# Moving one table in SBUF and regrouping rows in DRAM: a convolution followed by a Laplace-type spectral layer

## The chip, the cores and the metric

The kernel runs on one core of a Trainium2 chip. A core has five engines that run side by side, each through its own list of instructions: TensorE (PE, matrix products, with the loading of weights shown apart as PEld), VectorE (DVE), ScalarE (ACT), GpSimd (POOL) and SyncE (SP, which here only issues DMA transfers). Sixteen DMA engines move data between DRAM and SBUF, the on-chip memory of 128 partitions. [...] The metric is device time in microseconds (us) of the whole kernel; lower is better.

## The reference

All data are float32. `x` has 16 images of 16 channels of 256 by 256 points. Two residual layers follow each other, each on group-normalised input:

```python
x = x + _L0_conv_ref(_gn(x), L0_conv_weight)
x = x + _L1_conv_ref(_gn(x), ty, tx, weights_pole1, weights_pole2, weights_residue)

def _L1_conv_ref(x, ...):
    alpha = fft2(x)
    A = 1.0 / (omega1 - weights_pole1);  Bm = 1.0 / (omega2 - weights_pole2)
    S = einsum('ikpq,oikp,xikq->oxik', weights_residue, A, Bm)
    output_residue1 = einsum('biox,oxik->bkox', alpha, S)
    C = einsum('biox,oikp->bikpx', alpha, A)
    D = einsum('bikpx,xikq->bikpq', C, Bm)
    output_residue2 = einsum('bikpq,ikpq->bkpq', D, weights_residue)
    x1 = ifft2(output_residue1).real
    F = einsum('kbpq,bipz->kbiqz', output_residue2, E1)   # E1, E2: exp(pole * t)
    x2 = einsum('kbiqz,biqx->kizx', F, E2).real
    return x1 + x2 / Nx / Ny
```

`_gn` is a group norm over pairs of channels without scale. `_L0_conv_ref` comes to a 3 by 3 circular convolution over 16 channels. `_L1_conv_ref` takes a two-dimensional Fourier transform, mixes the 16 channels at each frequency with a weight built from poles and residues, adds a low-rank transient part, and transforms back.

## The kernel before

The kernel runs in four stages, one after the other, with scratch tensors in DRAM between them.

**Convolution** (`conv`, one call per step g, 24 steps per image, 384 in all). `load_x` brings an image in as two halves of 18 rows per partition, each in four loads (`PARTS`, `load_part`, L123); the loads for image b + 2 are issued while image b is convolved. Per step 16 pairs of matmuls (L294) run with 32 by 32 weights. Every six steps two PSUM tiles of rows `lo` and two of the mirrored rows `hi` are finished; ScalarE evicts them (L309) into `vt`. `mirror` then makes the sum and the difference of a row and its mirror image: the sum on VectorE into `vsum` (L261), the difference on GpSimd in place (L264); ScalarE squares both for the second norm (L272). The list `folded` says at which later step SP stores which half of them (L319) into `vD[b]`, one scratch tensor per image with the sums and the differences 2 MB apart. `x_stats` computes the first norm's statistics (L179) in pieces spread over the steps before an image. A generator, `tables`, is advanced by one `next` per step and builds the pole tables meanwhile: `make_hat` runs over two sides and two halves, loads `s_h` from `hD` for each (L439, eight loads that each fill 16 partitions with five rows of 2 KB), and a few steps later ScalarE squares it (L452). `make_c` writes the residues' table to `cD`.

**Fold** (64 units of a channel i and four images). `load_v` reads sums and differences of a unit into `s` (L729, one load per image, two units ahead; those of the first unit are issued by GpSimd), `fold` folds them along x on VectorE and GpSimd (L740 to L754), `lines` and `columns` transform them on PE (L762, L770, L790, L805) through the tile `t`, and VectorE and GpSimd write the spectrum `spec` of a channel, which is stored to `aD` (L961). Even and odd channels have a `spec` buffer of their own, and there are two buffers of `t`. The first weights of the next stage (`weights`, tiles `u` and `v`) are computed in its last units.

**Mix** (32 groups g). `ct` is loaded from `cD` in one transfer of 4 MB (L995). `sums` multiplies weights by `ct` on PE (L1017), `spread` copies the result into `sg` on ScalarE and VectorE (L1034, L1037), `mix` multiplies `sg` by `abd`, blocks of `aD` (L1087, L1092, L1105), and the results are evicted to `yt` and stored to `yD` (L1119). `first_sums` is the start of this stage: all four pieces of the first `sg` before the first `mix`.

**Last stage** (64 units of a channel k and four images). `load_v` reads the same sums and differences into `vl` (L1295), `combine` joins the halves of `yD` on GpSimd (L1312, L1316), `along_x` and `along_y` transform back (L1348, L1372, L1373), `put_out` adds `vl` (L1381), makes top and bottom rows from sum and difference (L1383, L1384) and stores them (L1386).

Pools of tiles are placed in SBUF one behind the other, and those of a new stage take bytes of the old one; the first write or load of a new tile waits for whoever last used any of its bytes. In this build `t` lies at 119,904 to 144,480 of each partition, even `spec` at 144,480 to 177,248, and `ct` at 142,368 to 175,136. An engine works through its list in order: a wait at its head holds up everything behind it, SP's DMA issues included.

Of the kernel before, what the change touches and what calls it, by code (L numbers as in the profile page):

```python
# [16 lines left out]
B = 16  # L17
# [7 lines left out]
def conv_then_laplace_kernel(ctx: ExitStack, tc: tile.TileContext, a: dict, out: bass.AP):  # L25
# [39 lines left out]

    vD = [dp.tile([2, P, C, N], FP, name=f"vD{b}", tag=f"vD{b}") for b in range(B)]
    aD = dp.tile([P, 2 * C, N * B], FP, name="aD", tag="aD")
# [41 lines left out]
    xp = p1.enter_context(tc.tile_pool(name="xt", bufs=5))  # L109
    vp = p1.enter_context(tc.tile_pool(name="vt", bufs=6))  # L110
    fp = p1.enter_context(tc.tile_pool(name="v_sums", bufs=2))
    jp = p1.enter_context(tc.tile_pool(name="junk", bufs=1))
# [6 lines left out]

    PARTS = 0, 5, 9, 14, 18  # L120

    def load_part(t, b, h, i, j):
        nc.sync.dma_start(out=t[:, i:j], in_=x[b][:, 16 * h + i : 16 * h + j])  # L123

# [133 lines left out]

    def mirror(g, b, u, lo, hi):
        both = fp.tile([P, 2, 2, N], FP, name="vsum", tag="vsum")  # L260
        nc.vector.scalar_tensor_tensor(  # L261
            both, lo, 1.0, hi, ALU.mult, ALU.add, accum_out=sums[:, b, u : u + 1]
        )
        nc.gpsimd.tensor_tensor(lo, lo, hi, ALU.subtract)  # L264
        folded.extend((g + 4 + 2 * j + r, b, u, j, t, r) for j, t in enumerate((both, lo)) for r in range(2))
        squared.append((g + 5, lambda: square(both, 4 + 2 * u, b, bias=shift2[:, b : b + 1])))
        squared.append((g + 7, lambda: square(lo, 5 + 2 * u, b)))

    def square(t, col, b, **by):

        junk = jp.tile([P, 4 * N], FP, name="junk", tag="junk")
        nc.scalar.activation(  # L272
            junk,
            t.rearrange("p r j x -> p (r j x)"),
            AF.Square,
            accum_out=sums[:, b, col : col + 1],
            **by,
        )

    def conv(g):  # L280


        for c in range(4):
            for r in range(4):
                at = g if r < 2 else g - 3
                if not 0 <= at < 24 * B:
                    continue
                b, u, n = at // 24, at // 6 % 4, at % 6
                phase, tap = n // 3, n % 3
                if n == 0 and c == 0:  # L290
# [3 lines left out]
                nc.tensor.matmul(  # L294
                    acc[r][32 * c : 32 * c + 32],
                    lhsT=ready[b][0][rows, phase, tap],
                    rhs=halves[b][u // 2][rows, q : q + 5 : 4, 2 - tap : 2 - tap + N],
                    start=n == 0,
                    stop=n == 5,
                )  # L300
        for r in (0, 1) if g % 6 == 5 else (2, 3) if g % 6 == 2 else ():
            at = g if r < 2 else g - 3
            if not 0 <= at < 24 * B:
                continue
            b, u = at // 24, at // 6 % 4
            if r % 2 == 0:
                vt = vp.tile([P, 2, 2, N], FP, name="vt", tag="vt")
                acc["v", r // 2] = vt
            nc.scalar.activation(vt[:, r % 2], acc[r], AF.Identity, bias=ready[b][1])  # L309
            if r == 3:  # L310
                later.append((g + 2, lambda g=g, b=b, u=u, lo=acc["v", 0], hi=vt: mirror(g, b, u, lo, hi)))
        while later and (later[0][0] <= g or g >= 24 * B + 2):
            later.pop(0)[1]()
        while squared and (squared[0][0] <= g or g >= 24 * B + 2):
            squared.pop(0)[1]()
        while folded and (folded[0][0] <= g or g >= 24 * B + 2):
            _, b, u, j, t, r = folded.pop(0)
            y = 64 * r + 16 * u
            nc.sync.dma_start(  # L319
                out=vD[b][j, y : y + 16].rearrange("(t y) c x -> (y c) t x", t=2),  # L320
                in_=t[:, r],
            )
# [96 lines left out]
    def make_hat(side):  # L419
# [13 lines left out]
        for half in range(2):  # L433
# [3 lines left out]
            at = slice(half * n, half * n + n)  # L437
            for p0 in range(0, P, 16):
                nc.sync.dma_start(  # L439
                    out=five[p0 : p0 + 16, 0:5],  # L440
                    in_=hD[0:5, side, :, at].rearrange("j a n -> a j n"),
                )
# [271 lines left out]
    prp = pool(p1, "prod", 2)  # L714
    bp = pool(p1, "b_const")
    pa = pool(p1, "p_y", 3, space=PSUM)
    px = pool(p1, "p_x", 4, space=PSUM)
# [139 lines left out]
    kp = pool(p2, "m_const", side="right")  # L857
    up = pool(p2, "uv", side="right")

# [20 lines left out]
    def weights(g):  # L880

        shape = [P, 32, 4]
        u = up.tile([P, 4, 32, 4], FP, name="u", tag="u")
        w, den, e, f = (u[:, j] for j in range(4))
        pr2, pre, pim = (prU[:, j].unsqueeze(2).to_broadcast(shape) for j in range(3))
        nc.vector.tensor_tensor(
            w,
            omg[:, g].unsqueeze(1).to_broadcast(shape),  # L890
            pims.unsqueeze(2).to_broadcast(shape),
            ALU.subtract,
        )
# [8 lines left out]
        v = up.tile([P, 32, 2, 4], FP, name="v", tag="v")  # L902
# [70 lines left out]
    wp = pool(p2, "w", 2)  # L973
    ep = pool(p2, "exps")
    a1 = pool(p2, "abd2")
    zp = pool(p2, "between")
# [62 lines left out]
    def first_sums():  # L1039
# [8 lines left out]
        sg = new_sg(0)  # L1048
        other = up.tile([P, 2, 2 * C], FP, name="other", tag="other")
        for h, w in enumerate((wt, w128)):  # L1050
# [328 lines left out]
    def put_out(k, b0, r, vl):  # L1379

        nc.vector.scalar_tensor_tensor(r, vl, 0.5, r, ALU.mult, ALU.add)  # L1381
        ol = op.tile([P, 2, 4, N], FP, name="ol", tag="ol")
        nc.vector.tensor_tensor(ol[:, 0], r[:, 0], r[:, 1], ALU.add)  # L1383
        nc.vector.tensor_tensor(ol[:, 1], r[:, 0], r[:, 1], ALU.subtract)  # L1384
# [28 lines left out]
    for n, (k, b0) in enumerate(units):  # L1413
# [7 lines left out]
        if n + 1 < len(units):  # L1421
# [4 lines left out]
            load_ahead(n + 1)  # L1426
        r = rp.tile([P, 2, 4, N], FP, name="r", tag="r")
        for j in range(4):
# [3 lines left out]
            if j == 0 and n:  # L1432
                put_out(*done)
            last = (ey_now[:, j], hs[:, j], pt, r[:, :, j], begun[j])
        done = (k, b0, r, v_now)
# [97 lines left out]
def _laid_out(x, L0_conv_weight, L1_conv_ty, L1_conv_tx, L1_conv_weights_pole1, L1_conv_weights_pole2, L1_conv_weights_residue):  # L1533
# [7 lines left out]
    rows = np.concatenate([np.pad(rows, ((0, 0), (0, 0), (1, 0))), np.pad(N - 1 - rows, ((0, 0), (0, 0), (0, 1)))])  # L1541
    g["x"] = xp[:, :, rows % N].transpose(0, 2, 3, 1, 4, 5).reshape(-1, P, 34, N + 2)
    w = np.asarray(L0_conv_weight)
# [52 lines left out]
```

## Time and profile before

| | us |
|---|---|
| median of 3 runs | 2668.16 |
| lowest and highest run | 2650.97, 2669.53 |
| the profiled execution's own time | 2673.96 |
| its span in the trace | 2672.0 |
| PE busy | 2486.5 (93%) |
| VectorE busy | 1994.7 (75%) |
| ScalarE busy | 1448.0 (54%) |
| GpSimd busy | 1311.7 (49%) |
| moved by DMA | 653.18 MB, 476,828 packets |

Times within the trace are counted from the start of the span. A group of instructions is named by its line, its engine and its operation, then output tile and input tiles. A number in brackets behind an instruction is the time that its engine had been idle, and what ended it; "issue" stands for an idle time whose end the profile can't put down to another engine. The chain of waits follows the work that ended last back through what released it. PE's clock is granted in windows; a figure below 1.00 means that some ran at half speed. The trace also has one record per DMA packet, with its size and duration.

### The profile page before, as it was taken

How to read it: one execution, taken by the hardware profiler on the slowest of the kernel's cores; microseconds unless marked ns; L12 is line 12 of the kernel's file. 1: busy time of each engine (PE TensorE's matmuls, PEld its weight loads, DVE VectorE, ACT ScalarE, POOL GpSimd, SP SyncE). 2: the span in 40 equal slices, each digit the busy share in tenths (PEclk: the TensorE clock that was granted, in tenths of full speed). 3: DMA queues.
4: the chain of work that ended last, by engine and by line, in shares of the span. 5: the costliest groups of instructions: out<-in, count | busy, mean ns of one | idle time of the engine just before them, and what ended most of it. 6: DMA issues, size and time to landing. Idle time of an engine off the chain costs nothing.

```text
span 2672.0 us, 84459 instructions
## 1 busy us (share of the span) xinstructions
PE 2486.5 (93%) x35314; PEld 1882.8 (70%) x35314; DVE 1994.7 (75%) x3805; ACT 1448.0 (54%) x2727; POOL 1311.7 (49%) x1181
## 2 busy tenths in 40 slices
PE   5988899889999999996999999999699999999998
PEld 2444454457777777774778878788588888888887
DVE  7767688848888888886777878888367666766666
ACT  2565566565666666664666656666244444444443
POOL 1333368433333333333466655676546565565653
PEclk9999999999999999998999999999899999999999
DMA  7888978855557656654777777777889989898985
GB/s 272 277 278 274 278 253 278 290 197 181 206 198 250 225 203 206 247 195 174 216 225 223 230 222 221 229 226 232 229 281 294 286 286 289 280 294 282 292 281 178
DMA packets 476828, 653.18 MB, mean 244 GB/s; under 512 B 51062, under 2 KB 426998, under 8 KB 466592
## 3 DMA queue, kind: packets, MB, share of 16 engines
q1 hardware_dynamic: 475376, 640.58, 74.6%
q8 instruction: 278, 4.55, 0.7%
q0 software_dynamic: 928, 3.02, 0.4%
q10 hardware_dynamic: 144, 4.19, 0.4%
q14 instruction: 102, 0.84, 0.1%
HBM read 368.15 MB, written 280.36 MB: 243 GB/s over the span
## 4 chain that ended last, share of the span: by engine, by line
PE 68%; DMA 12%; DVE 10%; SPq 5%; issue 3%; ACT 2%; POOL 0%; DVEq 0%; ACTq 0%; POOLq 0%
PE ps_conv L294 16%; PE ps_mix L1105 11%; PE ps_y L762 9%; PE ps_y L770 8%; PE ps_p L1348 5%; PE ps_x L805 4%; PE ps_f L1372 4%; PE ps_f L1373 4%; DMA yk<-yD 4%; DMA yD<-yt 3%; PE ps_s L1017 3%; DVE r L1381 2%; SPq L1119 2%; DMA out_y<-ol 2%; PE psd L790 1%
## 5 line engine op out<-in xcount | busy, mean ns | idle before, releaser
L1105 PE MATMUL ps_mix<-abd,sg 128*64 128x128 f32 x8192 | 484.5, 277 | 36.2 <-ACT yt L1218 14.5
L1105 PEld LDWEIGHTS ps_mix<-abd,sg 128*64 128x64 f32 x8192 | 454.4, 139 | 89.3 <-ACT yt L1218 47.8
L1312 POOL TENSOR_TENSOR u<-yk 128x512 f32<-128x512 f32 (+1 forms) x268 | 348.9, 1333 | 307.5 <-PE ps_p L1348 200.8
L294 PE MATMUL ps_conv<-xt,wc 32*32 32x512 f32 x12288 | 451.4, 618 | 48.5 <-issue 44.0
L294 PEld LDWEIGHTS ps_conv<-xt,wc 32*32 32x32 f32 x12288 | 252.6, 104 | 235.3 <-issue 157.9
L778 ACT ACTIVATE t<-ps_y,vmr 128x384 f32<-128x384 f32 x512 | 297.0, 580 | 163.9 <-PE ps_y L770 163.9
L1037 DVE STREAM_SHUFFLE sg<-ps_s 128x512 f32<-128x512 f32 (+1 forms) x264 | 328.8, 1317 | 0.0
L762 PE MATMUL ps_y<-tabE,vq 128*128 128x256 f32 x1024 | 313.5, 388 | 13.2 <-DVE vq L751 11.7
L264 POOL TENSOR_TENSOR vt<-vt 128x1024 f32<-128x1024 f32 x64 | 151.6, 2369 | 330.6 <-DVE vsum L261 268.5
L770 PE MATMUL ps_y<-tabO,vq 128*128 128x256 f32 x1024 | 306.4, 381 | 0.0
L1348 PEld LDWEIGHTS ps_p<-inv,u 128*128 128x128 f32 x2048 | 266.0, 193 | 50.2 <-issue 25.1
L1372 PE MATMUL ps_f<-pt,inv 128*128 128x256 f32 x1008 | 300.9, 380 | 0.0
L1373 PE MATMUL ps_f<-hs,ey 128*128 128x256 f32 x1008 | 300.0, 379 | 0.0
L1376 DVE TENSOR_TENSOR r<-ps_f,q 128x256 f32<-128x256 f32 x256 | 107.0, 418 | 252.4 <-ACT q L1375 252.4
L1348 PE MATMUL ps_p<-inv,u 128*128 128x128 f32 x2048 | 279.4, 280 | 13.2 <-POOL u L1316 13.1
L1034 ACT ACTIVATE sg<-ps_s,mcol 128x512 f32<-128x512 f32 (+1 forms) x264 | 179.5, 689 | 201.9 <-DVE sg L1037 117.9
L309 ACT ACTIVATE vt<-ps_conv,xq 128x512 f32<-128x512 f32 x256 | 161.9, 683 | 196.3 <-PE ps_conv L294 196.2
L762 PEld LDWEIGHTS ps_y<-tabE,vq 128*128 128x128 f32 x1024 | 189.8, 191 | 89.9 <-ACT q L818 51.2
L1375 ACT COPY q<-ps_f 128x256 f32<-128x256 f32 x256 | 95.4, 372 | 289.3 <-PE ps_f L1373 285.5
L750 POOL TENSOR_TENSOR vq<-vf 128x512 f32<-128x512 f32 x64 | 81.4, 1272 | 294.2 <-DVE vf L754 277.3
L1350 ACT COPY pt<-ps_p 128x512 f32<-128x512 f32 x256 | 150.1, 586 | 136.1 <-PE ps_p L1348 131.5
L770 PEld LDWEIGHTS ps_y<-tabO,vq 128*128 128x128 f32 x1024 | 195.7, 191 | 27.0
(238 smaller groups left out, 4072.1 us busy)
## 6 DMA issues: line engine op xcount, KB each, us to landing
yD<-yt SPq DMA_DIRECT2D x512, 128.0 KB, 3.5
vl<-vD SPq DMA_DIRECT2D x256, 256.0 KB, 4.0
out_y<-ol SPq DMA_DIRECT2D x128, 512.0 KB, 9.8
s<-vD SPq DMA_DIRECT2D x252, 256.0 KB, 5.9
aD<-spec SPq DMA_DIRECT2D x15, 4096.0 KB, 13.2
yk<-yD SPq DMA_DIRECT2D x60, 1024.0 KB, 8.7
xt<-in_x SPq DMA_DIRECT2D x64, 645.0 KB, 5.3
xt<-in_x SPq DMA_DIRECT2D x64, 516.0 KB, 7.0
```

Source lines behind the costliest of these rows:

```text
L294: nc.tensor.matmul(acc[r][32 * c : 32 * c + 32], lhsT=ready[b][0][rows, phase, tap], rhs=halves[b][u // 2][rows, q : q + 5 : 4, 2 - tap : ...
L309: nc.scalar.activation(vt[:, r % 2], acc[r], AF.Identity, bias=ready[b][1])
L762: nc.tensor.matmul(ps[:, 0:N], lhsT=vf[:, xo, 0, j], rhs=tabE[:, 0 : i + 2 : i + 1], start=True, stop=False, skip_group_check=True,)
L770: nc.tensor.matmul(ps[:, P : P + N], lhsT=vf[:, xo, 1, j], rhs=tabO[:, i : C + 1 : C - i], start=False, stop=True, skip_group_check=True,)
L778: nc.scalar.activation(t[:, xo, j].rearrange("p l n -> p (l n)"), ps[:, 0:384], AF.Copy, scale=vmr[:, 0, b0 + j, i : i + 1],)
L1034: nc.scalar.activation(to[..., k : k + 2], src[odd], AF.Copy, scale=nsgn)
L1037: nc.vector.stream_shuffle(to[..., C + k : C + k + 2], src[1 - odd], swap)
L1105: nc.tensor.matmul(ps[64 * t : 64 * t + 64, j], lhsT=sg[:, f : f + 2].rearrange("p f m -> p (f m)"), rhs=abd[jq][:, :, 2 * t + cc, 2 * jj ...
L1312: nc.gpsimd.tensor_tensor(u[:, :, j].rearrange("p b (c n) -> p c b n", c=8), in0, in1, o)
L1348: nc.tensor.matmul(ps[:, at], lhsT=u[:, n], rhs=tab, start=True, stop=True)
L1372: nc.tensor.matmul(ps[:, e], lhsT=tab, rhs=pt[:, e], start=True, stop=False)
L1373: nc.tensor.matmul(ps[:, e], lhsT=ey[:, e], rhs=hs, start=False, stop=True)
```

## The change

Four things change together.

- The single buffers `u` and `v` of `weights` leave the right end of SBUF: the first `u` sits in a pool `u0` of the fold, the later ones in a pool `u` below `abd2`. The tiles above it move up: `ct` now lies at 144,672 to 177,440.
- Sum and difference of a unit of the convolution share a tile `pair`, and `vD` is one tensor per four images in which a row of a channel holds, for four images, sum and difference side by side. A store writes runs of 2 KB, and `s` and `vl` are read in runs of 4 KB per partition, by two loads a unit. The output has the same order, by pairs of images.
- `x` is laid out in groups of two rows (2,064 bytes) with 16 bytes between them, and `PARTS` is made even.
- A batch of `s_h` is five loads over 128 partitions with a broadcast source, one per row, instead of eight over 16 partitions.

```diff
-    vD = [dp.tile([2, P, C, N], FP, name=f"vD{b}", tag=f"vD{b}") for b in range(B)]
+    vD = [dp.tile([P, C, 4, 2, N], FP, name=f"vD{b}", tag=f"vD{b}") for b in range(B // 4)]
...
-    vp = p1.enter_context(tc.tile_pool(name="vt", bufs=6))
-    fp = p1.enter_context(tc.tile_pool(name="v_sums", bufs=2))
+    vp = p1.enter_context(tc.tile_pool(name="v_pair", bufs=3))
+    fp = p1.enter_context(tc.tile_pool(name="v_far", bufs=2))
...
-    PARTS = 0, 5, 9, 14, 18
+    PARTS = 0, 4, 10, 14, 18

     def load_part(t, b, h, i, j):
-        nc.sync.dma_start(out=t[:, i:j], in_=x[b][:, 16 * h + i : 16 * h + j])
+        nc.sync.dma_start(
+            out=t[:, i:j].rearrange("p (n r) x -> p n (r x)", r=2),
+            in_=x[b][:, 8 * h + i // 2 : 8 * h + j // 2, 0 : 2 * (N + 2)],
+        )
...
-    def mirror(g, b, u, lo, hi):
-        both = fp.tile([P, 2, 2, N], FP, name="vsum", tag="vsum")
+    def mirror(g, b, u, pair, hi):
+        both, lo = pair[:, :, :, 0], pair[:, :, :, 1]
...
         nc.gpsimd.tensor_tensor(lo, lo, hi, ALU.subtract)
-        folded.extend((g + 4 + 2 * j + r, b, u, j, t, r) for j, t in enumerate((both, lo)) for r in range(2))
+        folded.extend((g + 7 + r, b, u, pair, r) for r in range(2))
...
-            nc.scalar.activation(vt[:, r % 2], acc[r], AF.Identity, bias=ready[b][1])
+            if r == 0:
+                pair = vp.tile([P, 2, 2, 2, N], FP, name="pair", tag="pair")
+                acc["v", 0] = pair, pair[:, :, :, 1]
+            elif r == 2:
+                far = fp.tile([P, 2, 2, N], FP, name="far", tag="far")
+                acc["v", 1] = far, far
+            to = acc["v", r // 2][1]
+            nc.scalar.activation(to[:, r % 2], acc[r], AF.Identity, bias=ready[b][1])
...
             nc.sync.dma_start(
-                out=vD[b][j, y : y + 16].rearrange("(t y) c x -> (y c) t x", t=2),
-                in_=t[:, r],
+                out=vD[b // 4][y : y + 16, :, b % 4].rearrange("(t y) c h x -> (y c) t (h x)", t=2),
+                in_=pair[:, r].rearrange("p t h x -> p t (h x)"),
             )
...
-            for p0 in range(0, P, 16):
+            for j in range(5):
                 nc.sync.dma_start(
-                    out=five[p0 : p0 + 16, 0:5],
-                    in_=hD[0:5, side, :, at].rearrange("j a n -> a j n"),
+                    out=five[:, j],
+                    in_=hD[j, side, :, at].unsqueeze(0).to_broadcast([8, 16, n]),
                 )
...
-        s = sp.tile([P, 2, 4, N], FP, name="s", tag="s")
-        for j in range(4):
-            eng.dma_start(
-                out=s[:, :, j], in_=vD[b0 + j][:, :, i, :].rearrange("h y x -> y h x")
-            )
-        return s
+        s = sp.tile([P, 4, 2, N], FP, name="s", tag="s")
+        for j in range(0, 4, 2):
+            eng.dma_start(out=s[:, j : j + 2], in_=vD[b0 // 4][:, i, j : j + 2])
+        return s.rearrange("p b h x -> p h b x")
...
-    up = pool(p2, "uv", side="right")
+    up = {"v": pool(p2, "v", side="right"), "u0": u0}
...
-        u = up.tile([P, 4, 32, 4], FP, name="u", tag="u")
+        u = up["u" if g else "u0"].tile([P, 4, 32, 4], FP, name="u", tag="u")
...
     ep = pool(p2, "exps")
+    up["u"] = pool(p2, "u")
     a1 = pool(p2, "abd2")
...
-        vl = vp.tile([P, 2, 4, N], FP, name="vl", tag="vl")
-        for j in range(4):
-            nc.sync.dma_start(
-                out=vl[:, :, j], in_=vD[b0 + j][:, :, k, :].rearrange("h y x -> y h x")
-            )
+        vl = vp.tile([P, 4, 2, N], FP, name="vl", tag="vl")
+        for j in range(0, 4, 2):
+            nc.sync.dma_start(out=vl[:, j : j + 2], in_=vD[b0 // 4][:, k, j : j + 2])
...
-        for h in range(2):
-            nc.sync.dma_start(
-                out=out[k, b0 : b0 + 4, h].rearrange("b y x -> y b x"), in_=ol[:, h]
-            )
+        for j in range(0, 4, 2):
+            nc.sync.dma_start(out=out[k, b0 // 4, :, j : j + 2], in_=ol[:, j : j + 2])
```

The host's preparation of `x` and its reading of the output follow the new order; both only move data.

More of the change, by code (lines that the diff above doesn't have):

```diff
@@ L269, in square @@
     def square(t, col, b, **by):
-        junk = jp.tile([P, 4 * N], FP, name="junk", tag="junk")
+        junk = jp.tile([P, 4, N], FP, name="junk", tag="junk")
         nc.scalar.activation(
             junk,
-            t.rearrange("p r j x -> p (r j x)"),
+            t.rearrange("p r j x -> p (r j) x"),
             AF.Square,
@@ L305, in conv @@
             b, u = at // 24, at // 6 % 4
-            if r % 2 == 0:
-                vt = vp.tile([P, 2, 2, N], FP, name="vt", tag="vt")
-                acc["v", r // 2] = vt
-            nc.scalar.activation(vt[:, r % 2], acc[r], AF.Identity, bias=ready[b][1])
+            if r == 0:
[6 more added lines that the diff above has]
+            nc.scalar.activation(to[:, r % 2], acc[r], AF.Identity, bias=ready[b][1])
             if r == 3:
-                later.append((g + 2, lambda g=g, b=b, u=u, lo=acc["v", 0], hi=vt: mirror(g, b, u, lo, hi)))
+                later.append((g + 2, lambda g=g, b=b, u=u, pair=acc["v", 0][0], hi=to: mirror(g, b, u, pair, hi)))
         while later and (later[0][0] <= g or g >= 24 * B + 2):
@@ L316, in conv @@
         while folded and (folded[0][0] <= g or g >= 24 * B + 2):
-            _, b, u, j, t, r = folded.pop(0)
+            _, b, u, pair, r = folded.pop(0)
             y = 64 * r + 16 * u
             nc.sync.dma_start(
-                out=vD[b][j, y : y + 16].rearrange("(t y) c x -> (y c) t x", t=2),
-                in_=t[:, r],
+                out=vD[b // 4][y : y + 16, :, b % 4].rearrange("(t y) c h x -> (y c) t (h x)", t=2),
+                in_=pair[:, r].rearrange("p t h x -> p t (h x)"),
             )
@@ L715, in conv_then_laplace_kernel @@
     bp = pool(p1, "b_const")
+    u0 = pool(p1, "u0")
     pa = pool(p1, "p_y", 3, space=PSUM)
@@ L901, in weights @@
         yield
-        v = up.tile([P, 32, 2, 4], FP, name="v", tag="v")
+        v = up["v"].tile([P, 32, 2, 4], FP, name="v", tag="v")
         nc.vector.tensor_tensor(v[:, :, 0], e, den, ALU.mult)
@@ L1048, in first_sums @@
         sg = new_sg(0)
-        other = up.tile([P, 2, 2 * C], FP, name="other", tag="other")
+        other = up["u"].tile([P, 2, 2 * C], FP, name="other", tag="other")
         for h, w in enumerate((wt, w128)):
@@ L1381, in put_out @@
         nc.vector.scalar_tensor_tensor(r, vl, 0.5, r, ALU.mult, ALU.add)
-        ol = op.tile([P, 2, 4, N], FP, name="ol", tag="ol")
-        nc.vector.tensor_tensor(ol[:, 0], r[:, 0], r[:, 1], ALU.add)
-        nc.vector.tensor_tensor(ol[:, 1], r[:, 0], r[:, 1], ALU.subtract)
-        for h in range(2):
-            nc.sync.dma_start(
-                out=out[k, b0 : b0 + 4, h].rearrange("b y x -> y b x"), in_=ol[:, h]
-            )
+        ol = op.tile([P, 4, 2, N], FP, name="ol", tag="ol")
+        nc.vector.tensor_tensor(ol[:, :, 0], r[:, :, 0], r[:, :, 1], ALU.add)
+        nc.vector.tensor_tensor(ol[:, :, 1], r[:, :, 0], r[:, :, 1], ALU.subtract)
+        for j in range(0, 4, 2):
+            nc.sync.dma_start(out=out[k, b0 // 4, :, j : j + 2], in_=ol[:, j : j + 2])
     units = [(k, b0) for k in range(C) for b0 in range(0, B, 4)]
@@ L1426, in conv_then_laplace_kernel @@
             load_ahead(n + 1)
-        r = rp.tile([P, 2, 4, N], FP, name="r", tag="r")
+        r = rp.tile([P, 4, 2, N], FP, name="r", tag="r")
         for j in range(4):
@@ L1433, in conv_then_laplace_kernel @@
                 put_out(*done)
-            last = (ey_now[:, j], hs[:, j], pt, r[:, :, j], begun[j])
+            last = (ey_now[:, j], hs[:, j], pt, r[:, j], begun[j])
         done = (k, b0, r, v_now)
@@ L1541, in _laid_out @@
     rows = np.concatenate([np.pad(rows, ((0, 0), (0, 0), (1, 0))), np.pad(N - 1 - rows, ((0, 0), (0, 0), (0, 1)))])
-    g["x"] = xp[:, :, rows % N].transpose(0, 2, 3, 1, 4, 5).reshape(-1, P, 34, N + 2)
+    xr = xp[:, :, rows % N].transpose(0, 2, 3, 1, 4, 5).reshape(-1, P, 17, 2 * (N + 2))
+    g["x"] = np.pad(xr, ((0, 0), (0, 0), (0, 0), (0, 4)))
     w = np.asarray(L0_conv_weight)
@@ L1589 @@
         args[name] = nc.dram_tensor(f"in_{name}", v.shape, mybir.dt.from_np(v.dtype), kind="ExternalInput").ap()
-    out = nc.dram_tensor("out_y", (C, B, 2, P, N), FP, kind="ExternalOutput").ap()
+    out = nc.dram_tensor("out_y", (C, B // 4, P, 4, 2, N), FP, kind="ExternalOutput").ap()
     with tile.TileContext(nc) as tc:
@@ L1593 @@
     r = run_bass_kernel_spmd(nc, [arrays], core_ids=[0])
-    y = r.results[0]["out_y"].transpose(1, 0, 2, 3, 4)
+    y = r.results[0]["out_y"].transpose(1, 3, 0, 4, 2, 5).reshape(B, C, 2, P, N)
     return np.concatenate([y[:, :, 0], y[:, :, 1, ::-1]], 2)
```

## The prediction

> **What bounds the kernel now.** I first cut the span into its stages (busy microseconds by engine in each stretch, then the granted clock, the DMA share and GB/s).
>
> ```profile
> 47.00:592.00 545.00, 488.26 (x12304) 267.57 (x12299) 393.21 (x790) 327.92 (x593) 248.77 (x188) 0.97 0.82 266
> 592.00:602.00 10.00, 2.19 (x5) 1.31 (x5) 4.26 (x10) 1.48 (x3) 2.48 (x2) 0.50 1.07 355
> 602.00:1218.00 616.00, 615.50 (x4096) 443.15 (x4096) 524.28 (x1205) 372.55 (x644) 221.02 (x281) 1.00 0.58 207
> 1218.00:1254.00 36.00, 14.09 (x288) 8.50 (x296) 19.66 (x88) 10.14 (x33) 11.34 (x8) 0.72 0.68 264
> 1254.00:1895.00 641.00, 604.79 (x12176) 514.72 (x12160) 504.04 (x905) 407.06 (x680) 389.62 (x298) 0.98 0.76 223
> 1895.00:1938.00 43.00, 24.32 (x197) 20.30 (x184) 15.99 (x16) 10.62 (x26) 29.67 (x43) 0.84 0.82 228
> 1938.00:2662.00 724.00, 718.53 (x5936) 617.41 (x5928) 494.32 (x686) 312.95 (x742) 408.60 (x360) 1.00 0.88 279
> ```
>
> The first busy figure is PE. Fold (602 to 1218) and the last stage (from 1938) have no PE time to give: what the change saves on DMA there is hidden. Time can be won in three seams (592, 1218, 1895) and in the convolution, where PE idles 545 − 488 = 57 us and 3% of the clock, some 16 us, is missing.
>
> Seam at 1218: the chain of waits, then the SP queue's own waits, then VectorE's timeline.
>
> ```profile
> 1217.94 18.16 DMA ct<-cD
> 1236.24 5.92 PE ps_s L1017 x96
> ...
> 1254.43 3.75 PE ps_mix L1105 x64
> ```
> ```profile
> SPq L1087 <- DMA aD<-spec: 23.6, 1, 23.6
> SPq L995 <- PE ps_x L805: 19.3, 1, 19.3
> SPq L995 <- DMA aD<-spec: 12.0, 1, 12.0
> ```
> ```profile
> 1225.97 0.69 DVE L1047 TENSOR_TENSOR accs<-proj 128x512 f32<-128x512 f32 x1 [3.64 <-POOL proj L851]
> 1238.33 0.73 DVE L1037 STREAM_SHUFFLE sg<-ps_s 128x256 f32<-128x256 f32 x1
> ```
>
> `ct` (4 MB) is issued only when the fold's last matmul has read `t`; 18 us pass before PE goes on. The load had been first in SP's queue, and had nothing else to wait for, 19.3 us earlier.
>
> Convolution: PE's gaps (in brackets, with no releaser) against SP's timeline.
>
> ```profile
> 143.45 10.44 PE L294 MATMUL ps_conv<-xt,wc 32*32 32x512 f32 x256 [3.60 <-issue]
> 219.95 8.09 PE L294 MATMUL ps_conv<-xt,wc 32*32 32x512 f32 x170 [3.60 <-issue]
> 291.23 9.00 PE L294 MATMUL ps_conv<-xt,wc 32*32 32x512 f32 x195 [4.21 <-issue]
> ```
> ```profile
> 131.60 3.64 SPq L439 DMA_DIRECT2D s_h<-hD  x8
> 203.45 3.71 SPq L439 DMA_DIRECT2D s_h<-hD  x8
> 275.78 3.64 SPq L439 DMA_DIRECT2D s_h<-hD  x8
> ```
>
> The three longest gaps (in brackets: idle just before the row's start) end 12 to 16.5 us after a batch of eight `s_h` loads is issued; the batches' packets run for 11 to 12 us. In the trace's DMA records a 16 KB packet of the instruction queue starts in each of these gaps and PE resumes 2.4 to 3.5 us after it: PE seems to wait for its instructions, which come late behind that batch. The batches' 2,048-byte packets take 250 ns each, those of that size elsewhere 84.
>
> [...] the trace has medians of 46 ns for 1,024 bytes, 84 for 2,048, 160 for 4,128, 199 for 5,160: 8 ns, and 38 per KB. [...] (`s` reads rows 16 KB apart at 46 ns).
>
> **The change, part by part**, against the profiled execution (2673.96 us; span 2672.0).
>
> *ct (−10.5).* `ct` moves from 142,368 to 144,672 in each partition, off `t` (ends at 144,480) and onto even `spec` alone, whose last store SP issues at 1186.28 and which lands 12.0 later, at 1198.6. 4 MB in 32 KB packets of 1,255 ns on 16 engines are 10 us and some 2 to land: about 1211, before PE needs it. What is late next is VectorE: its accs at 1225.97 wait for GpSimd's proj and stand ahead of the shuffles, which can begin at 1226.7, not 1238.33: 11.7 gained. The `aD` store of the last channel (issued 1221.69) then runs alone, 13.2 by its row, to 1235 instead of 1242; the four `abd` loads behind it (2.5 to issue, 4.3 to land) come at 1241.5, just before the mix at 1254.4 − 11.7 = 1242.7. PE idles in between, so a few us of half clock may return: 10.5 (7 to 13).
>
> *s_h (−7).* 32 loads become 20[...]. Gaps tied to the four batches: 2.79 (before 73.42), 3.60, 1.79 (before 211.83), 3.60 and 4.21, 16 in all; after each the clock record shows a window of 3.4 us at half speed, 1.7 lost, so 24 with the clock. [...] I take 7, because the batch still takes as long and ScalarE's next instruction on `s_h` (idle up to 2.96 for it, with the evictions queued behind) still waits. Ends: −25, all of it gone, and +10, each of four batches 2.5 us longer.
>
> *x (+0.8 at the start, hidden later).* A half image per partition: 2 × 199 + 2 × 160 = 718 ns now, 9 × 85 = 765 after; 47 × 128/16 = 0.38 us per half. Two halves stand ahead of `wband` (lands 15.36), on which VectorE waits. Later loads run two images ahead. The small packets may shorten the queue before an instruction fetch: bound below by case B.
>
> *vD stores (0; 0 to +15).* 256 of 256 KB become 128 of 512 KB: 256 × 84 for 512 × 46 ns, 0.13 us less of 16 engines each; SP loses half its issues (0.4 each) and its waits on the sum (99.8), which nobody on the path waits for. New: sums and differences both leave at steps g+7 and g+8 (g+4 to g+7 before), and the pair's buffer is rewritten by ScalarE 7 steps after the last, 8 before. A step is 545/384 = 1.42 us: 9.9 us against landings of 6.0 median, 8.5 at most, plus 1.3 for the double size. It just fits; behind a late one stand ScalarE's evictions, then PE with two spare banks.
>
> *Seam at 592 (−3; −5 to 0).* Unit 0's loads, four of 0.74 us on GpSimd, arrive at 590.65, 592.7, 594.5 and 595.83, each awaited; two contiguous ones should be there by 592.5. SP's last stores stay ahead of later units.
>
> *Fold and last stage (0; −1 to +2).* `s`, `vl` and `out` go from 1 KB to 4 KB packets. Per last-stage unit 2048 × 46 becomes 512 × 160: 12 of 16 engine-us, 0.8 us of 11.4, beside a full PE. If that cover were gone it would be a gain. VectorE and ScalarE keep their counts and sizes; strides change, bound ±1.
>
> *Seam at 1895 (−1; −4 to +2).* Two fewer vl issues (0.5 each) before the `yk` loads. *Tail (+0.5; 0 to +1.5).* Both output stores now wait for the second `ol` (1.2 us): 1 MB behind the last instruction instead of 0.5, about 1.3 more, less the cheaper packets.
>
> Sum: 0.8 − 7 − 3 − 10.5 − 1 + 0.5 = −20.2: 2654 by the profiled execution. The median shown is 5.8 below that: **2648**.
>
> **Rivals.** *A*, the above. *B, the convolution opens:* all PE gaps without releaser there are 44.0 us in 27 waits, and 16 of clock; if fetches wait behind bytes in the queue, 2 KB packets of x in place of 5 KB ones cut most of them. Two thirds, 40, in place of 7: 2615. For it: the packets of x, a third of the DMA time there, fall from 199 and 160 ns to 85. Against: vD packets double, the traffic stays. *C, slower: HBM rows.* Reads of `vD` now step 128 KB between partitions, stores 8 KB. If a 4 KB packet of `vl` took more than about 300 ns (floor 160), the last stage, with 12% of DMA left, turns DMA-bound; at 400 it is (400 − 300) × 256/16 = 1.6 us a unit, × 64 = +100: 2748. Against: the 8 KB packets of `yk`, at a pitch of 512 KB, have a median of 328, where 8 + 8 × 38 gives 312. *D, given back:* ScalarE waits for the pair's stores (+15)[...], ct stays: 2668 − 13 + 20 = 2675; with a late store in every unit, 64 × 0.7, over 2695. *E, it doesn't do what it says:* `ct` is issued no sooner: 2658. The waits that the built program gives it name an `aD` store and the convolution's last matmuls and evictions, not the fold's, so hardly.
>
> **How the numbers follow.** A 0.53, B 0.18, C 0.05, D 0.20 (0.06 of it over 1%), E 0.04. A run of this kernel varies by 0.7%, so 1% is about what can be told from no change: 2641.5 and 2695. Faster: B, and 0.14 of A's lower end: 0.32. Slower: C and 0.06: 0.11. Same: 0.57. Range 2620 to 2676, which leaves out C, D's worst and part of B. A's own range is 2636 to 2660.
>
> **What would show it.** Right: SP issues `ct` some 19 us before the fold's last matmul instead of right after it; VectorE's idle of 11.67 before the first shuffle is gone, and the stretch from the fold's last matmul to the first mix is about 26 us instead of 36; fold still 616 us, last stage 724; DMA share there near 0.81; gaps after the s_h batches halved. Wrong: ScalarE's evictions waiting for DMA in the convolution (D); vl packets over 300 ns (C); gaps without releaser below 20 us in all (B).

## The result, and the profile after

The changed kernel takes 2667.47 us (median of 12 runs, 2658.88 to 2672.8); the kernel before takes 2664.31 us (12 runs beside it). The ratio is 1.001, 95% interval 0.9993 to 1.0027: a difference that can't be told from none, where a gain of 20 us was forecast.

The profiled execution of the changed kernel took 2667.82 us, with a span of 2665.7 us. Its stages are cut at the end of the convolution, the first matmul of the fold, its last one, the first and the last mix, and some 40 us behind that. Columns: stretch, length, busy us of PE, of its weight loads, VectorE, ScalarE, GpSimd (instructions in brackets), granted clock, DMA share, GB/s.

```profile
47.00:597.00 550.00, 491.39 (x12306) 270.52 (x12304) 386.16 (x787) 324.76 (x587) 244.40 (x184) 0.97 0.79 260
597.00:609.00 12.00, 0.00 (x0) 0.00 (x0) 4.47 (x10) 4.63 (x8) 3.09 (x3) 0.62 0.98 338
609.00:1228.20 619.20, 617.28 (x4108) 444.31 (x4115) 522.63 (x1200) 373.12 (x644) 223.43 (x283) 0.99 0.56 215
1228.20:1253.60 25.40, 13.93 (x297) 8.07 (x296) 24.21 (x98) 10.18 (x33) 12.21 (x8) 0.80 0.52 209
1253.60:1891.50 637.90, 601.24 (x12152) 511.31 (x12158) 505.52 (x903) 407.04 (x680) 389.88 (x298) 0.99 0.76 224
1891.50:1932.00 40.50, 25.16 (x208) 20.81 (x205) 15.76 (x15) 10.62 (x26) 29.27 (x42) 0.86 0.90 254
1932.00:2655.50 723.50, 720.24 (x5936) 618.46 (x5936) 489.85 (x689) 312.07 (x742) 422.22 (x360) 1.00 0.81 278
```

The prediction cut the kernel before at round times, up to 5.4 us behind these events. Cut at the events themselves, its first, second and fourth stretches are:

```profile
47.00:586.60 539.60, 488.26 (x12304) 267.57 (x12299) 390.75 (x787) 324.14 (x587) 243.68 (x184) 0.97 0.82 266
586.60:598.30 11.70, 0.05 (x1) 0.08 (x1) 5.60 (x10) 4.69 (x8) 5.09 (x5) 0.65 0.96 310
...
1217.84:1254.35 36.51, 14.44 (x296) 8.50 (x296) 20.14 (x90) 10.18 (x33) 11.85 (x8) 0.72 0.67 260
```

Two stretches have changed by more than a few microseconds, in opposite directions. The one from the fold's last matmul to the first mix is 25.4 us instead of 36.5. The convolution ends at 597.0 instead of 586.6. So the gain was there, and the convolution had given up about as much 600 us earlier. The other differences (2 us each in the mix, the seam behind it and the last stage) are no larger than those between executions of one code: the mix took 640.2 us in the profile of before and 633 to 637 in those of the experiments, and the last stage, from its first matmul to its last, between 742 and 754. That is also why the two profiled spans differ by -6.3 us while the medians differ by +3.2.

First the gain. The SP queue around `ct` (timeline), its waits, and VectorE (timeline), all of the changed kernel:

```profile
1208.02 0.32 SPq L1002 DMA_DIRECT2D ct<-cD  x1
```
```profile
SPq L1094 <- DMA aD<-spec: 34.9, 1, 34.9
...
SPq L1002 <- DMA aD<-spec: 11.0, 1, 11.0
...
SPq L1002 <- ACT t L784: 0.2, 1, 0.2
```
```profile
1236.93 0.68 DVE L1054 TENSOR_TENSOR accs<-proj 128x512 f32<-128x512 f32 x1
...
1237.54 0.72 DVE L1044 STREAM_SHUFFLE sg<-ps_s 128x256 f32<-128x256 f32 x1
```

`ct` is issued 20.2 us before the fold's last matmul ends (1228.2) and no longer after it. SP waits 11.0 us for the `aD` store with it and 0.2 us for one of ScalarE's evictions into `t`; the wait of 19.3 us for the fold's last matmul is gone. The first shuffle follows right behind `accs`; the 11.67 us of idle between them are gone. The chain of waits of the changed kernel shows what ends last in this seam now (start, duration; pieces under 0.5 us are left out):

```profile
1231.51 1.20 DVE pr L856 x2
1232.70 0.90 DVE u L894
1233.63 1.25 DVE u L900
...
1235.22 0.95 DVE u L903
...
1237.01 0.54 DVE accs L1054
1237.55 0.54 DVE sg L1044
...
1239.10 3.77 PE ps_s L1024 x64
```

No transfer is in it any more. VectorE's own work is what is late next.

Then the loss. PE's group of convolution matmuls in the list of groups (busy us, mean ns | idle before them, by what ended it), before and after:

```profile
L294 PE MATMUL ps_conv<-xt,wc 32*32 32x512 f32 x12288 | 451.4, 618 | 48.5 <-issue 44.0 <-DVE wc L237 4.1
```
```profile
L297 PE MATMUL ps_conv<-xt,wc 32*32 32x512 f32 x12288 | 453.0, 618 | 57.6 <-issue 49.6 <-DVE wc L240 4.1 <-ACT pair L316 3.6
```

The matmuls themselves take as long (453.0 against 451.4). The idle before them has grown by 9.1: 5.6 more without a releaser, and 3.6 new behind ScalarE's evictions into `pair`. This profile doesn't say which part of the change does that.

### The profile page after: what moved, and what is told of

It is laid out like the page before. It is cut to its first block, busy times and chain, and to the rows that moved or that the text cites. A ratio compares the mean times of both kernels' runs of the same rounds, so it can differ in the third digit from the quotient of the medians.

```text
span 2665.7 us, 83901 instructions
## 1 busy us (share of the span) xinstructions
PE 2487.3 (93%) x35314; PEld 1883.0 (71%) x35314; DVE 1986.5 (75%) x3805; ACT 1447.7 (54%) x2727; POOL 1324.7 (50%) x1179
## 4 chain that ended last, share of the span: by engine, by line
PE 63%; DMA 4%; SPq 3%; DVE 3%; ACT 1%; issue 1%; POOL 1%; DVEq 0%; ACTq 0%; POOLq 0%
PE ps_mix L1112 11%; PE ps_y L768 9%; PE ps_p L1353 9%; PE ps_y L776 8%; PE ps_f L1377 8%; PE ps_f L1378 8%; PE ps_x L811 4%; DMA yD<-yt 3%; PE ps_s L1024 3%; PE ps_h L1337 2%; SPq L1126 2%; PE psd L796 1%; SPq L1094 1%; DVE sg L1044 1%; ACT yt L1225 0%
## 5 line engine op out<-in xcount | busy, mean ns | idle before, releaser
L297 PE MATMUL ps_conv<-xt,wc 32*32 32x512 f32 x12288 | 453.0, 618 | 57.6 <-issue 49.6
L267 POOL TENSOR_TENSOR pair<-pair,far 128x1024 f32<-128x1024 f32 x64 | 151.6, 2369 | 345.8 <-DVE pair L264 285.6
L1225 ACT COPY yt<-ps_mix 128x512 f32<-128x512 f32 x352 | 184.8, 591 | 51.2 <-DMA yD<-yt 35.2
```

Of the source, the lines that this page charges most:

```text
L297: nc.tensor.matmul(acc[r][32 * c : 32 * c + 32], lhsT=ready[b][0][rows, phase, tap], rhs=halves[b][u // 2][rows, q : q + 5 : 4, 2 - tap : ...
L1225: (nc.vector.tensor_copy if m >= (2 if late else 3) else nc.scalar.copy)(o, src)
```

## The experiments

Three sizes come back in every run. *Gaps* is the idle without releaser in the group of convolution matmuls. *Stores' packets* are the DMA records of the size of a `vD` store's rows (1 KB or 2 KB), from 330 us (behind the last `s_h` batch) to the end of the convolution: their mean and their 95th percentile, which one in twenty exceeds, in ns. The records don't name a tensor; about one in eight of the 1 KB packets belongs to something else. The convolution's length is from its first matmul to the end of its last. Each run has one profile, which gives all but its median and its ratio.

| run | what it has of the change | median us | ratio to before (95%) | convolution us | gaps us | stores' packets ns |
|---|---|---|---|---|---|---|
| before | nothing | | 1 | 557.6 | 44.0 | 1 KB: 47.8, 52 |
| changed | all | 2667.5 | 1.0010 (0.9993 to 1.0027) | 567.6 | 49.6 | 2 KB: 99.8, 184 |
| e1 | ct | 2655.1 | 0.9957 (0.9940 to 0.9973) | 556.8 | 45.6 | 1 KB: 47.9, 54 |
| e2 | x | 2666.9 | 1.0006 (0.9988 to 1.0025) | 555.0 | 41.5 | 1 KB: 47.9, 53 |
| e3 | s_h | 2661.5 | 0.9986 (0.9973 to 0.9999) | 554.8 | 37.3 | 1 KB: 47.8, 52 |
| e4 | vD and output regrouped | 2689.0 | 1.0085 (1.0061 to 1.0109) | 583.9 | 65.0 | 2 KB: 102.4, 195 |
| e5 | none; stores in one burst | 2670.7 | 1.0010 (0.9993 to 1.0027) | 562.3 | 46.1 | 1 KB: 48.6, 67 |
| e6 | e4, stores apart | 2684.0 | 1.0062 (1.0037 to 1.0087) | 576.2 | 64.0 | 1 KB: 51.8, 85 |
| e7 | ct, x, s_h | 2647.8 | 0.9927 (0.9898 to 0.9956) | 555.2 | 39.0 | 1 KB: 47.6, 52 |
| e8 | all, stores apart | 2659.1 | 0.9973 (0.9958 to 0.9988) | 564.4 | 52.5 | 1 KB: 52.0, 88 |
| e9 | only vD's places in HBM | 2687.2 | 1.0071 (1.0046 to 1.0096) | 573.7 | 62.3 | 1 KB: 52.0, 86 |
| e10 | all, vD by image | 2651.7 | 0.9934 (0.9911 to 0.9958) | 555.8 | 36.5 | 2 KB: 91.6, 145 |
| e11 | e6, old places of vD | 2668.2 | 0.9993 (0.9976 to 1.0010) | 555.3 | 42.5 | 1 KB: 48.0, 53 |
| e12 | all, vD padded | 2649.8 | 0.9943 (0.9920 to 0.9965) | 558.8 | 39.5 | 2 KB: 90.9, 140 |

**One part at a time.** Four kernels, each the kernel before with one part of the change: e1 the pools of `u`, e2 `x`, e3 the `s_h` loads, e4 the rest (`vD`, its tiles, stores and loads, and the output). Their diffs are the hunks of the change.

> The kernel before with only the pools of u changed, so that ct moves. Theory (the gain at 1218 is whole, and the convolution of the changed kernel gives it back): ratio 0.996, 10 to 11 us less; fold's last matmul to first mix 25.5 us instead of 36.5; convolution as before. Rival (it is given back later, in the mix, whatever the convolution does): ratio 0.999 to 1.001.

> The kernel before with only x in groups of two rows and its PARTS. Theory that the packets of x cost the convolution: the wait for instructions in it grows by 5 us or more, ratio 1.002 to 1.004. Theory that the stores of pairs do it: ratio 0.999 to 1.001, PE's gaps without releaser in the convolution near the 44 us of before.

> The kernel before with only the s_h loads as broadcasts, 20 for 32. Forecast on record: 7 us less (ratio 0.997), gaps after the batches halved from 16 us. Rival: nothing, since a batch still takes 11 us (ratio 1.000); or +5 us, if the batch holds up the x loads behind it.

> The kernel before with only the regrouping of vD and the output (pairs, 4 KB rows). Theory that the pair stores give the gain back: convolution 8 to 12 us longer, with ScalarE waiting for stores into the pair some 4 to 7 us and PE gaps without releaser above 48 us; ratio 1.003 to 1.005. Theory that x does it: ratio 0.998 to 1.000.

e1 keeps its whole gain: 11 us off the median, and 26.5 us from fold to mix; the rival falls. e2 does nothing that can be measured. e3 gains 0.14%, some 4 us, about half of what was forecast, with an interval from 0 to 7. e4 alone costs 0.85%, 23 us, more than the others gain and about twice what was expected of it: the loss is in the regrouping. The trace of e4 has it in the convolution, which is 26 us longer, with 65.0 us of gaps. ScalarE's waits are not it: PE idles 1.3 us behind them.

```profile
L294 PE MATMUL ps_conv<-xt,wc 32*32 32x512 f32 x12288 | 453.2, 615 | 70.5 <-issue 65.0 <-DVE wc L237 4.1 <-ACT pair L313 1.3
```

The four ratios add up to +9 us, the whole change measures +3; with intervals of 3 to 6 us each way for each part, that is no contradiction.

**Burst or place?** My theory was then that a megabyte stored at once delays PE's instruction fetches. e5 puts such a burst into the kernel before, made of that kernel's own stores:

```diff
-folded.extend((g + 4 + 2 * j + r, b, u, j, t, r) for j, t in enumerate((both, lo)) for r in range(2))
+folded.extend((g + 7 + r, b, u, j, t, r) for r in range(2) for j, t in ((1, lo), (0, both)))
```

e6 takes the burst away from e4, and e8 from the changed kernel, leaving the new tiles and places:

```diff
-folded.extend((g + 7 + r, b, u, pair, r) for r in range(2))
+folded.extend((g + 4 + 2 * j + r, b, u, j, t, r) for j, t in enumerate((both, lo)) for r in range(2))
...
-    out=vD[b // 4][y : y + 16, :, b % 4].rearrange("(t y) c h x -> (y c) t (h x)", t=2),
-    in_=pair[:, r].rearrange("p t h x -> p t (h x)"),
+    out=vD[b // 4][y : y + 16, :, b % 4, j].rearrange("(t y) c x -> (y c) t x", t=2),
+    in_=t[:, r],
```

e7 is the kernel before with `ct`, `x` and `s_h`.

> The kernel before, its 256 KB stores of 1 KB rows unchanged in size and place, but each unit's four issued together behind GpSimd's subtraction (difference first, at steps g+7 and g+8) instead of the sums at g+4 and g+5. Theory (a megabyte in one burst delays PE's instruction fetches): convolution 15 to 26 us longer, PE gaps without releaser 60 to 68 us, ratio 1.006 to 1.009. Rival (the 2 KB rows, or the new addresses, cost it): convolution as before within 4 us, ratio 0.999 to 1.001.

> The kernel with only the regrouping of vD and output, but sums and differences stored apart as before (256 KB each, 1 KB rows, sums at g+4 and g+5, differences at g+6 and g+7) into the new places. Theory (burst): convolution within 4 us of before, gaps near 47 us, ratio 0.998 to 1.001 instead of the 1.0085 of the pair stores. Rival (new addresses in HBM, or ScalarE's buffers held longer): convolution still 15 us or more longer, ratio 1.005 or more.

> The changed kernel without the regrouping of vD and output: ct, x and s_h alone. If the parts add: -11.1 + 0.7 - 3.7, ratio 0.9945 to 0.9955. If x gains only beside the pair stores, as the changed kernel's 2667 against 2689 - 11 - 3 suggests, the same; if it gains beside s_h, 0.992 or less.

> The changed kernel with only the stores taken apart (256 KB, 1 KB rows, sums first, as before). Theory (burst): 12 to 16 us under the changed kernel, ratio 0.994 to 0.997 against before, convolution 553 to 559 us. Rival (buffers or addresses): no better than the changed kernel, ratio 0.999 to 1.002.

The theory fell on both sides. The burst alone costs 3 us (interval -2 to +7), with a convolution 5 us longer and 2 us more of gaps; without it the new layout still costs 0.62%, with 64.0 us of gaps. Storing apart does help the changed kernel (e8: 0.9973, an interval clear of the changed kernel's), but by 8 us instead of 12 to 16. e7 is at 0.9927: nothing but the regrouping stands between the change and its gain.

What e6 and e8 share with e4, and e5 lacks, shows in the packets: the 1 KB packets of e6 and e8 have the same median as ever (46 ns), but one in twenty takes 85 ns or more instead of 52. Either the tile in SBUF or the place in HBM could do that. e9 changes only the place, in the kernel before, e11 only the tiles (and the output), e10 keeps the tiles and the joint stores but lays `vD` out image by image, so that each store is one unbroken block:

```diff
e9, against the kernel before
-vD = [dp.tile([2, P, C, N], ...) for b in range(B)]
+vD = [dp.tile([P, C, 4, 2, N], ...) for b in range(B // 4)]
-                out=vD[b][j, y : y + 16].rearrange("(t y) c x -> (y c) t x", t=2),
+                out=vD[b // 4][y : y + 16, :, b % 4, j].rearrange("(t y) c x -> (y c) t x", t=2),
-                out=s[:, :, j], in_=vD[b0 + j][:, :, i, :].rearrange("h y x -> y h x")
+                out=s[:, :, j], in_=vD[b0 // 4][:, i, j]
...
e10, against the changed kernel
-vD = [dp.tile([P, C, 4, 2, N], ...) for b in range(B // 4)]
+vD = [dp.tile([P, C, 2, N], ...) for b in range(B)]
-                out=vD[b // 4][y : y + 16, :, b % 4].rearrange("(t y) c h x -> (y c) t (h x)", t=2),
+                out=vD[b][y : y + 16].rearrange("(t y) c h x -> (y c) t (h x)", t=2),
-        for j in range(0, 4, 2):
-            eng.dma_start(out=s[:, j : j + 2], in_=vD[b0 // 4][:, i, j : j + 2])
+        for j in range(4):
+            eng.dma_start(out=s[:, j], in_=vD[b0 + j][:, i])
...
```

(`vl` is read in the same way as `s`. e11 is e6 with the `vD` of before, and reads from it as before.)

> The kernel before with only vD's places in HBM changed: its own SBUF tiles, its own 256 KB stores and 256 KB loads, but sums and differences of four images side by side, so that a store's 1 KB rows lie 8 KB apart instead of one behind the other. Theory (scattered rows: packets of the stores are served more slowly, 52 ns mean against 48, with a 95th percentile of 85 against 52, and fetches wait with them): convolution 14 to 20 us longer, gaps above 60 us, ratio 1.005 to 1.007. Rival (the tile in SBUF that holds both and is freed later): convolution as before, ratio 0.999 to 1.001.

> The changed kernel with vD laid out image by image: pair tile and 512 KB stores of 2 KB rows as in the changed kernel, but each store one unbroken block of HBM; s and vl are read by image, four loads of 2 KB rows a unit. Theory (scattered rows): 12 to 19 us under the changed kernel, ratio 0.993 to 0.996 against before, 95th percentile of the stores' packets near the 85 ns median. Rival (pair tile or burst): as the changed kernel, ratio 0.999 to 1.002.

> The kernel before with only the pair tiles in SBUF (three of 8 KB and two of 4 KB, rows of sums and differences interleaved) and the output's regrouping; separate 256 KB stores into the old places, read back from there as before. Theory (scattered rows): convolution within 4 us of before, ratio 0.998 to 1.001. Rival (pair tile): 14 to 20 us longer, ratio 1.005 to 1.007.

All three came out for the place. e9, with the same instructions and the same bytes moved as the kernel before, costs 0.71%, 19 us, and shows e6's gaps and packets. Its group of convolution matmuls:

```profile
L294 PE MATMUL ps_conv<-xt,wc 32*32 32x512 f32 x12288 | 451.9, 613 | 66.7 <-issue 62.3 <-DVE wc L237 4.1
```

e11 is the kernel before to 0.07%. e10 is 0.9934: the changed kernel with its tiles and stores, and without its loss. Its group, and one of ScalarE's waits in its convolution, with the same wait of the changed kernel (total, times, longest) behind it:

```profile
L297 PE MATMUL ps_conv<-xt,wc 32*32 32x512 f32 x12288 | 450.0, 614 | 46.1 <-issue 36.5 <-ACT pair L316 5.2 <-DVE wc L240 4.1
```
```profile
ACT pair L316 <- DMA vD<-pair: 6.7, 3, 2.4
```
```profile
ACT pair L316 <- DMA vD<-pair: 6.8, 4, 2.0
```

The wait for the pair's stores is real, but the kernel that is 20 us faster by the ratios (0.9934 against 1.0010) has it as well. It isn't what costs. One expectation was missed: e10's 95th percentile is 145, not near 85, so only a part of the changed kernel's 184 is due to the place.

The gaps say the same in all fourteen profiles. Without those in the 20 us behind each `s_h` batch, they come to 23 to 29 us in the nine profiles without the new places or with e12's padding (below), and to 37 to 48 us in the five with them.

**Why this place?** A store's pieces lie 8 KB apart in the changed `vD` (four images of 2 KB), a power of two. If that distance is what costs, another one ends the loss; if scatter as such does, it stays. e12 adds one row of 1 KB that nothing uses, so that they lie 9 KB apart, still in separate pieces:

```diff
-vD = [dp.tile([P, C, 4, 2, N], ...) for b in range(B // 4)]
+vD = [dp.tile([P, C, 9, N], ...) for b in range(B // 4)]
-                out=vD[b // 4][y : y + 16, :, b % 4].rearrange(
+                out=vD[b // 4][y : y + 16, :, 2 * (b % 4) : 2 * (b % 4) + 2].rearrange(
-            eng.dma_start(out=s[:, j : j + 2], in_=vD[b0 // 4][:, i, j : j + 2])
+            eng.dma_start(out=s[:, j : j + 2].rearrange("p b h x -> p (b h) x"), in_=vD[b0 // 4][:, i, 2 * j : 2 * j + 4])
...
```

> The changed kernel with one unused row of 1 KB added to each group of vD, so that the 2 KB pieces of a store lie 9 KB apart instead of 8 (a power of two); stores, tiles and 4 KB loads unchanged. Theory[...]: 12 to 17 us under the changed kernel, ratio 0.993 to 0.996 against before, convolution near 556 us, 95th percentile of the stores' packets under 150 ns. Theory that scattered pieces as such are slow: no change, ratio 0.999 to 1.002, 95th percentile near the 184 ns of the changed kernel.

```profile
L297 PE MATMUL ps_conv<-xt,wc 32*32 32x512 f32 x12288 | 451.5, 614 | 47.9 <-issue 39.5 <-DVE wc L240 4.1 <-ACT pair L316 4.0
```

0.9943, as e7 and e10 within their intervals: one unused row in nine takes the loss away, with as many separate pieces. So the cost depends on the distance and doesn't come from scatter as such. That the power of two is what matters is not shown: there is this one pair of distances. The padding also moves other things that no run separates: the two pieces of each partition lie 1.125 MB instead of 1 MB apart (another power of two), and what lies behind `vD` in DRAM may have moved. e7, e10 and e12 beat the kernel before by 15 to 20 us and the changed kernel by 18 to 22; which of them is best these runs can't tell.

The traces place 9 to 12 us of that in the convolution (567.6 us in the changed kernel, 555.2 to 558.8 in these three). They can't place the rest: one profile each, and the last stage alone differs by up to 12 us between profiles, whatever the layout.

## Why the prediction was wrong

**The failing step** is "vD stores (0; 0 to +15)". It priced the stores by count and size of packets ("256 × 84 for 512 × 46 ns") and by whether a landing fits ("9.9 us against landings of 6.0 median"). Both prices assume that a packet of a given size takes a given time wherever it goes. In the new places the stores' 2 KB packets kept a median of 85 ns, but their mean was 99.8 where the padded layout has 90.9, and the idle of PE without a releaser grew. The term is +18 us: the changed kernel against e12, (1.0010 − 0.9943) × 2666; against e7 it is +22, and e9 gives +19 on its own. That is above the step's upper end of 15, which was put there for another mechanism.

An estimate from these figures: 128 stores have 32,768 packets of 2 KB; 8.9 ns more for each are 18 us of sixteen engines' time, as much as was lost. For e9 it is 65,536 packets at 4.2 ns, 17 us, where 19 were lost. For e8 it is 18 us too, but against e7 it lost only 12, and the DMA share of the convolution is 0.79 in the changed kernel and 0.85 in e9. So that PE pays for this time one for one is not shown.

Two sentences of the prediction came close. Rival C named the new HBM rows and even "stores 8 KB", but looked for the cost at the reads, in the last stage. The 4 KB packets there, of `vl` and of the output together, have a median of 159 ns and a mean of 177 (forecast 160); the DMA share fell to 0.81, as forecast; nothing is lost (749.9 us from the stage's first matmul to its last, against 751.5). Rival D had the stores of the pair and nearly the number (2675), but the number by luck: its mechanism was ScalarE's wait, which e10 shows to be harmless. And I had taken the pitch of the new places as harmless. What a trace showed of pitches was of reads alone: `s` reads rows 16 KB apart at 46 ns a packet, `yk` 8 KB packets 512 KB apart at 328. For stores of 1 and 2 KB pieces 8 KB apart, beside other traffic, these runs show otherwise (95th percentile 86 instead of 52 ns in e9), and a pitch of 9 KB took the loss away (e12: 0.9943).

That the loss shows at PE, which reads nothing of `vD` in the convolution, seems to go by the route that the prediction described for `s_h`: waiting for instructions. The traces show when the packets and the gaps come, not that one causes the other. The instruction queue moved 278 packets of 16 KB for PE's 70,628 instructions, one for about 256, and many of PE's rows between two gaps are 128 weight loads and 128 matmuls. Of its gaps over 1 us without a releaser, 18 before the convolution matmuls of before became 28 in e9's, and a packet of that queue starts 2 to 4 us ahead of the end of every one of them; of arbitrary points in that time, about 35% have one so placed. The queue's line in the page of before (packets, MB), and two of e9's rows behind gaps:

```profile
q8 instruction: 278, 4.55, 0.7%
```
```profile
144.94 4.51 PE L294 MATMUL ps_conv<-xt,wc 32*32 32x512 f32 x128 [3.34 <-issue]
151.13 4.50 PE L294 MATMUL ps_conv<-xt,wc 32*32 32x512 f32 x128 [1.69 <-issue]
```

Why such packets would come later beside these stores is open; no run tests it.

Point by point:

- *ct, −10.5*: right in mechanism and size. The seam became 11.1 us shorter, e1 gained 11. `ct` was issued 20.2 us ahead of the fold's end (19 forecast), and what is late next is VectorE's work, as forecast.
- *s_h, −7*: right in sign; e3 gave −4, with −7 at the edge of its interval. That half of the gaps' time could be spared was my estimate, which no trace of before showed. In a batch of e3 about 8 packets are under way at a time (their durations added up, over the batch's run) where the kernel before has 14, and the batch again takes 10 to 12 us, as the prediction had it. What was mis-sized is the share spared. Gaps that end in the 20 us behind the start of a batch are 11 to 13 us in the six profiles with the new loads (12.8 in the changed kernel) and 16 to 20 in the eight with the old ones (16.3 before): some 5 us, a third and not half. The clock's part was misread, too: of the five gaps that the prediction lists, the one before 211.83 has no window of half speed behind it, and the last has a double one. PE's rows of the changed kernel, with three of the gaps ahead of them:

```profile
148.76 7.03 PE L297 MATMUL ps_conv<-xt,wc 32*32 32x512 f32 x148 [3.70 <-issue]
...
221.21 8.11 PE L297 MATMUL ps_conv<-xt,wc 32*32 32x512 f32 x173 [2.77 <-issue]
...
294.37 4.51 PE L297 MATMUL ps_conv<-xt,wc 32*32 32x512 f32 x127 [2.12 <-issue]
```

- *x, +0.8 at the start*: +0.4 (the first convolution matmul at 29.4 instead of 29.0), and nothing later. Rival B, which hoped for small packets of `x`, is out: 41.5 us of gaps in e2 against 44.0.
- *Seam at 592, −3*: it gave nothing. The seam is 12.0 us instead of 11.7. In the timeline of the changed kernel, unit 0's two loads land together no earlier than the four did:

```profile
596.38 1.38 POOL L737 DMA_DIRECT2D s<-vD  x2
...
597.47 3.27 SPq L737 DMA_DIRECT2D s<-vD  x3
...
602.70 0.61 DVE L746 SCALAR_TENSOR_TENSOR vf<-s,vmr 128x128 f32<-128x128 f32 x2 [3.18 <-DMA s<-vD]
...
606.34 0.61 DVE L746 SCALAR_TENSOR_TENSOR vf<-s,vmr 128x128 f32<-128x128 f32 x2 [3.03 <-DMA s<-vD]
```

  The second is in 10.0 us after the issue, where the last of four had taken 9.7. Seven transfers of 512 KB share the engines here (unit 0's two loads on GpSimd's queue; two stores and three more loads on SP's). The view of before had said so: DMA share 1.07 at 355 GB/s in this stretch of it. Fewer waits shortened nothing there.
- *Fold and last stage, 0*: right (619.2 us against 619.6; the last stage's stretch 723.5 against 724). *Seam at 1895, −1*: the mix's end to the first `ps_p` is 13.1 us against 15.4, but also 13.5 to 15.6 in e1 to e3, which leave this part as it was; no effect told from noise. *Tail, +0.5*: +0.6, 11.2 us behind PE's last matmul instead of 10.6.

With −4 for `s_h`, 0 for the seam at 592 and +18 for the stores, the prediction's own sum becomes 0.4 − 4 − 11.1 + 0.5 + 18 = +4 (the seam at 1895 taken as 0, too); measured was +3, interval −2 to +7.

## What to carry to other kernels

When a layout in HBM changes, work out the distance between the pieces of every store as well as of every load, and put a bound on what it may cost instead of taking it as free. The one costly distance here was 8 KB, and a spare row of 1 KB per group was a cheap test and the cure (1.0010 became 0.9943). Where PE waits with no releaser in the profile, a slower transfer that it never reads can be what it pays for (62.3 us of such waits in e9, 44.0 before, with only the places of `vD` changed), so look at the mean and the tail of the packet times and not at their median (e9: 46 ns as before, with a 95th percentile of 86 instead of 52). And in the seam at 592, whose DMA share was already 0.96, fewer and larger transfers gave nothing back (11.7 us before, 12.0 after).

## What the runs showed of the hardware

- Stores whose 1 KB pieces lie 8 KB apart kept the median of 46 ns a packet, while the 95th percentile rose from 52 to 86 ns (e9); the convolution beside them lost 16 us. With 2 KB pieces, 8 KB apart: 99.8 ns on average and 184 at the 95th percentile; 9 KB apart: 90.9 and 140 (e12); in one block: 91.6 and 145 (e10).
- Storing 1 MB at once instead of in two halves cost 8 us where the pieces lay 8 KB apart (changed kernel against e8; e4 against e6 has 5, within the intervals), and within the intervals nothing where they did not (e10 and e12 against e7; e5 against before).
- A batch of `s_h` as eight loads over 16 partitions each had 14 packets of 2 KB under way at a time, at 226 to 250 ns each (three of the four batches of before; the one issued from 131.60 moved 1.31 MB in 11.1 us, 118 GB/s); as five broadcast loads over 128 partitions 7 to 8, at 97 to 146 ns (e3), and took as long.
- With `ct` waiting at the head of SP's list, SP issued nothing from 1186.61 to 1217.94 in the kernel before: 12.0 us for the `aD` store, then 19.3 for the fold's last matmul. The `abd` loads behind it came at 1242.14.
- The granted clock was 1.0 or 0.5 throughout: in the profile of before, 18 windows of 3.4 to 20.5 us at 0.5, in that of the changed kernel 18 of 3.4 to 17.1. The one between fold and mix was 20.5 us long before and 10.2 in the changed kernel.
